# Groups of nodes that fit 17 slots of edges, found on chip, in place of blocks of 128 nodes, in a two-layer graph attention kernel

## The chip, the cores and the metric

One Trainium2 chip, one core. The metric is the device time of one execution in microseconds; a run is one execution, and the time of a kernel is the median of its runs.

## What is computed

Two layers of relational graph attention over 3125 nodes with 768 features, then a residual and a layer norm. There are 53125 edges, sorted by the node they point at (`dst`), each of one of 3 types. Every node has an edge to itself, so no node is empty; a node has 17.0 edges in the mean.

```python
def rgat_conv(x, W, q, k, b, src, dst, etype, heads, out_ch, n_nodes):
    xr = jnp.einsum('nd,rdf->rnf', x, W)          # three products per node, one per edge type
    oi = xr[etype, dst]
    oj = xr[etype, src]
    qi = oi @ q
    kj = oj @ k
    alpha = jax.nn.leaky_relu(qi + kj, NEG_SLOPE)
    m = jax.ops.segment_max(alpha, dst, num_segments=n_nodes)
    e = jnp.exp(alpha - m[dst])
    z = jax.ops.segment_sum(e, dst, num_segments=n_nodes)
    a = e / (z[dst] + EPS)
    msg = (a[:, :, None] * oj.reshape(-1, heads, out_ch)).reshape(-1, heads * out_ch)
    return jax.ops.segment_sum(msg, dst, num_segments=n_nodes) + b

h = rgat_conv(x, W1, q1, k1, b1, src, dst, edge_type, 4, 192, n)
h = jax.nn.elu(h)
out = rgat_conv(h, W2, q2, k2, b2, src, dst, edge_type, 1, 768, n)
x = _layernorm(x + out)
```

## The kernel before

The nodes are cut into NB = 25 blocks of P = 128 (the last has 53). Since the edges are sorted, the edges of a block stand together. They are taken in slots of 128 edges, one edge per partition: SL = 18 slots for each of the first 24 blocks, SLL = 9 for the last, NK = 441 in all. A block with more edges than its slots hold raises `flag`, and then a general kernel, which stands behind a test at the end of the program, does everything again.

The order of the instructions on every engine is written out by hand (`tc.manual_schedule`). What the program says first on an engine runs first there. A dictionary `ev` lists what is to be issued at each step of a pass.

**Preparation** (`prepare`, `weights_kq`, `nodes_kq`). The edge lists are brought to DRAM (`ed_d`: source row, scaled target, type, and whether the target changes; `dr_d`: target modulo 128). For each of the 26 block borders DVE counts the edges that lie before it (L205), so that `starts` holds where each block's edges begin. Meanwhile W1 is split into two parts of short mantissa (`wH`, `wL`), and each node's attention keys and queries for all types and heads are worked out: keys go to a table `kt1` in DRAM, queries to `qq` in SBUF. `first` makes block 0's rows of the first table.

**Pass 1** (`phase1`). Its steps n are the products of x with W1, `d_group(b, r, c)`: block b, type r, half c of the 768 outputs, 18 matmuls of 128x384 each (L629). Six of them make a block's rows of the first table `tab1`; ACT copies each out of PSUM (L641), SP stores them (L643). There are 144 steps and a few behind them. Between them stands the attention of layer 1. For block b, counted from step 6b: `a_load` (its edge list, SP) and `a_load2` at -9; `a_index` (a PE transpose, L516) at -6; `a_index2` (DVE makes the gather list `ridx`, L520 to L526) and 18 gathers of keys (`a_gathers`, POOL, L451, into one of three tiles `kt`) at -5; `a_q`, `a_q2`, `a_q3` (each edge's query, by a product of a one-hot matrix with the block's queries) at +1 to +3; `a_alpha` (DVE, L565, which needs all keys of the block) at +4; `a_max`, `a_scan` (maxima over each node's edges by two scans), `a_back`, `a_put` (weights into `pall`) at +5 to +8. For the blocks below 8, the steps from +4 on come two later. The last block has a list of its own (`last`), since pass 2 begins with it. W2 is split and stored beside this, and loaded over W1's place in the last 24 steps.

**Pass 2** (`phase2`). Its steps k are the slots. `gather(k)` (POOL, L451) brings 128 rows of 772 numbers of `tab1` into one of nine tiles `share`. `high` scales them by the weights per head (ACT, L788) and makes the 0/1 matrix `sel` that adds edges to nodes (POOL, L790, in two slots of three; DVE in the third). `low` makes the rest of the scaled rows (DVE, L802). `sums` adds into the block's PSUM (PE, L821, four matmuls). When a block is complete, e_y to e_s2 apply bias and ELU and transpose it, and `d_part` multiplies it with W2 (PE, L876, 108 matmuls, 18 parts spread over the slots of the next block). `d_row` copies the rows out (L884) and SP stores them in `tab2` (L890). The blocks go in the order 24, 0, 1, ..., 23.

**Pass 3** (`phase3`). The same over `tab2` for layer 2, with the attention of a block (a_load to a_put) worked out between the slots. The rows go into six tiles `G` of six slots (PART). The sums (L1090) follow the gathers by LAG = SL + 11 slots. At the end of a block the residual is added, normalised (e_y to e_low), and SP stores the result (`e_out`, L1130).

All gathers are issued by one helper, so they have one line:

```python
G.indirect_dma_start(out=to, out_offset=None, in_=tab, in_offset=_index(i[:, j:j + 1]), ...)   # L451
steps = ((-9, a_loads), (-9, a_loads2), (-6, a_index), (-5, a_index2), (-5, a_gathers), (1, a_q), (2, a_q2),
         (2, a_window), (3, a_q3), (4, a_alpha), (5, a_max), (6, a_scan), (7, a_back), (8, a_put))
order = [NB - 1, *range(NB - 1)]       # pass 2
LAG = SL + 11                          # pass 3
```

Of the kernel before, what the change touches and what calls it, by code (L numbers as in the profile page):

```python
# [37 lines left out]
SL = 18  # L38
CAP = SL * P

SLL = 9

FRONT = 256
BACK = CAP + 256

PART = 6
# [5 lines left out]
def kernel(  # L52
# [8 lines left out]
):  # L61

# [26 lines left out]
    NK = (NB - 1) * SL + SLL  # L89
# [5 lines left out]
    first_rows = {0: 0, 1: 1, 2: 2, NB - 1: 3}  # L95
# [4 lines left out]
    tab2 = dram.tile([NP * R, RW], F32, name="ftab2")  # L100
    kt1 = dram.tile([NP * R, 4], F32, name="kt1")
    xb_d = dram.tile([NP, D], F32, name="xb_d")
# [11 lines left out]
    starts = keep.tile([1, 32], I32, name="starts")  # L114
# [3 lines left out]
    dl = keep.tile([P, NB, SL], F32, name="fdl")  # L118
    rel = keep.tile([P, NB, SL], F32, name="rel")
    pall = keep.tile([P, NB, SL, H1], F32, name="pall")  # L120
    q1s = keep.tile([P, NB, H1, R, 3], BF, name="q1s")
# [48 lines left out]
    def prepare(work, bank, wide, half):  # L170
# [7 lines left out]
        cnt = work.tile([EP, 32], F32, name="cnt")  # L178
        V.memset(cnt, 0.0)
# [20 lines left out]
        blk = tile_(I32)  # L200
        V.tensor_single_scalar(blk, di, 7, op=ALU.logical_shift_right)
        bb, junk, dr = (half[:EP, i * ET:(i + 1) * ET] for i in range(3))
        V.tensor_copy(bb, blk)
        for b in range(NB + 1):
            V.tensor_scalar(junk, bb, float(b), 0.0, op0=ALU.is_lt, op1=ALU.add, accum_out=cnt[:, b:b + 1])  # L205
            yield
            if b == 10:
                win = wide[:EP, :ET + P]
                c = ed_d[1:2, FRONT:FRONT + 1]
                G.dma_start(win, bass.AP(tensor=c.tensor, offset=c.offset, ap=[[ET, EP], [1, ET + P]]))  # L210
                rx = tile_(F32)
                V.scalar_tensor_tensor(rx, si, float(R), ti, op0=ALU.mult, op1=ALU.add)
                store(ed_d[0], rx)
                yield
                tf = tile_(F32)
                V.tensor_copy(tf, ti)
                store(ed_d[2], tf)
                yield
                V.tensor_single_scalar(di, di, P - 1, op=ALU.bitwise_and)
                V.tensor_copy(dr, di)  # L220
                store(dr_d[0], dr)
                yield
# [3 lines left out]
        V.tensor_reduce(cnt[:, 30:31], junk, AX.X, ALU.add)  # L226
        yield
        V.tensor_tensor(junk, dB, win[:, P:ET + P], op=ALU.is_equal)
        V.tensor_reduce(cnt[:, 31:32], junk, AX.X, ALU.add)
# [8 lines left out]
        T.matmul(pc[:1, :32], ones, cnt, start=True, stop=True)  # L238
        cf = work.tile([1, 32], F32, name="cf")
        V.tensor_copy(cf, pc[:1, :32])  # L240
        V.tensor_copy(starts, cf)
        yield
        big = work.tile([1, 32], F32, name="big")
        V.tensor_sub(big[:, :NB], cf[:, 1:NB + 1], cf[:, 0:NB])
        V.tensor_scalar(big[:, :NB - 1], big[:, :NB - 1], float(CAP), None, op0=ALU.is_gt)
        V.tensor_scalar(big[:, NB - 1:NB], big[:, NB - 1:NB], float(SLL * P), None, op0=ALU.is_gt)
        V.tensor_copy(big[:, 30:32], cf[:, 30:32])
        V.memset(big[:, NB:30], 0.0)
        tot = work.tile([1, 1], F32, name="tot")
        V.tensor_reduce(tot, big, AX.X, ALU.add)  # L250
        V.tensor_copy(flag, tot)
# [90 lines left out]
    def nodes_kq(buf, pre, work, psum, bank, wk, kqs, wH, wL, qq, more, edges_ready):  # L342
# [86 lines left out]
        for m in range(1, NCH + 2):  # L429
            if m >= NCH:  # L430
                place(m - 2, prod.pop(m - 2))
            elif m > 1:
                got[m] = turn(m)
            fill(fills[m])
            if 0 <= m - 1 < NCH:
                prod[m - 1] = product(m - 1, got[m - 1])
            more(3)
            if m == NCH - 3:
                edges_ready()
                x_load(pre, 1)  # L440
        yield

    ends = {min((b + 1) * SL, NK) - 1 for b in range(NB)}
# [1300 lines left out]
```

## Time and profile before

| | us |
|---|---|
| median of three runs | 2289.55 |
| lowest and highest run | 2287.75, 2296.72 |
| the profiled execution | 2285.11 |
| its span, from the first to the last instruction | 2283.3 |
| first gather of keys | 124.46 |
| first sum of pass 2 | 743.85 |
| first gather of pass 3 | 1608.82 |

Busy time over the span: PE 2049.8 us (90%), PE's weight loads 1765.0 (77%), DVE 1555.7 (68%), ACT 1401.7 (61%), POOL 1733.3 (76%). The mean granted clock of PE was 0.95 of full speed.

How to read the lines that follow: "L451 POOL DMA_INDIRECT kt<-kt,ridx x378 | busy, mean ns | idle before <-what ended it" is a group of like instructions; a gather through `rfirst` instead of `ridx` is the same operation for blocks 0, 1, 2 and 24. A line of the waits is "engine line waited for: total us, times, longest us". In a timeline a line begins with the start and the duration in us. PE is TensorE, PEld its weight loads, DVE VectorE, ACT ScalarE, POOL GpSimd, SPq the queue of SyncE.

### The profile page before, as it was taken

The page shows a single profiled execution, that of the slowest core. Times are in us where ns is not written, and L with a number is a line of the kernel's source. Part 1 is how long each engine was busy: PE and PEld are TensorE (multiplying, and loading weights), DVE is VectorE, ACT ScalarE, POOL GpSimd, SP SyncE. Part 2 cuts the span into 40 slices and gives each one's busy share as a digit, 9 for nine tenths or more (in the row PEclk, how much of TensorE's full clock was granted, in tenths as well). Part 3 has the DMA queues.
Part 4 walks back from the last instruction along what each step waited for, and adds up shares of the span by engine and source line. Part 5 has one row for each costly group of instructions (what it writes and reads, how often), then busy time and mean ns, then how long its engine had stood idle before and what let it go on. Part 6 is the DMA issues. An engine that isn't in the chain of part 4 may idle for free.

```text
span 2283.3 us, 37563 instructions
## 1 busy us (share of the span) xinstructions
PE 2049.8 (90%) x11055; PEld 1765.0 (77%) x11055; DVE 1555.7 (68%) x4075; ACT 1401.7 (61%) x3197; POOL 1733.3 (76%) x1685
## 2 busy tenths in 40 slices
PE   6998988898886899999999999999489999899986
PEld 5888888888886799999999999999255555565554
DVE  7734434343432899999999999996266666676666
ACT  5411111111111788888888888885278888787885
POOL 4267777777776888888888888884677777777772
PEclk9989998999998899999999999999699999999998
DMA  6554544454455877777777777776788888888881
GB/s 181 178 149 164 170 145 145 161 170 145 159 184 158 308 245 234 233 230 235 234 235 237 228 233 240 236 233 219 256 283 298 298 306 299 288 273 281 278 289 65
DMA packets 153595, 508.22 MB, mean 223 GB/s; under 512 B 40404, under 2 KB 53723, under 8 KB 153383
## 3 DMA queue, kind: packets, MB, share of 16 engines
q0 software_dynamic: 85472, 334.19, 48.2%
q1 hardware_dynamic: 57681, 155.56, 19.0%
q10 hardware_dynamic: 10230, 15.98, 2.2%
q8 instruction: 91, 1.49, 0.3%
q14 instruction: 121, 0.99, 0.1%
HBM read 428.40 MB, written 94.04 MB: 229 GB/s over the span
## 4 chain that ended last, share of the span: by engine, by line
PE 38%; POOL 7%; DMA 6%; issue 6%; DVE 6%; ACT 4%; POOLq 0%; DVEq 0%; ACTq 0%
PE po L876 14%; PE acc L821 11%; PE acc L1090 10%; DMA G<-ftab,ridx 5%; POOL share L451 3%; POOL sel L790 2%; DVE L L802 2%; POOL G L451 1%; ACT H L1068 1%; DVE L L1079 1%; PE pt L851 1%; DMA G<-ftab,rfirst 1%; DMA share<-ftab,ridx 1%; PE pa L1020 0%; PE bc L977 0%
## 5 line engine op out<-in xcount | busy, mean ns | idle before, releaser
L788 ACT ACTIVATE H<-share,pall 128x193 fp32r<-128x193 f32 x1748 | 642.7, 447 | 104.9 <-DMA share<-ftab,ridx 36.6
L802 DVE SCALAR_TENSOR_TENSOR L<-share,pall,H 128x193 fp32r<-128x193 f32 x1748 | 648.6, 437 | 25.2 <-ACT H L788 17.7
L876 PE MATMUL po<-wH,hT 128*128 128x386 f32 (+1 forms) x1800 | 532.8, 339 | 0.0
L451 POOL DMA_INDIRECT G<-ftab,ridx x378 | 421.9, 1116 | 115.2 <-issue 58.8
L451 POOL DMA_INDIRECT kt<-kt,ridx x378 | 405.2, 1072 | 115.1 <-issue 113.9
L451 POOL DMA_INDIRECT share<-ftab,ridx x378 | 428.1, 1133 | 81.3 <-DVE L L802 42.0
L629 PE MATMUL po<-wH,xT 128*128 128x384 f32 x1584 | 444.1, 353 | 0.7 <-ACT xT L615 0.7
L1090 PE MATMUL acc<-G,selp 128*128 128x386 f32 x904 | 357.0, 521 | 0.3 <-ACT selp L1064 0.3
L876 PEld LDWEIGHTS po<-wH,hT 128*128 128x128 f32 x1800 | 334.4, 189 | 0.6 <-DVE hT L864 0.5
L876 PE MATMUL po<-wL,hT 128*128 128x386 f32 (+1 forms) x900 | 304.7, 339 | 0.0
L629 PEld LDWEIGHTS po<-wH,xT 128*128 128x128 f32 x1584 | 301.3, 196 | 3.4 <-issue 0.8
L641 ACT COPY share<-po 128x384 f32<-128x384 f32 x144 | 68.9, 479 | 337.0 <-PE po L629 267.2
L629 PE MATMUL po<-wL,xT 128*128 128x384 f32 x792 | 274.7, 347 | 0.0
L821 PE MATMUL acc<-H,sel 128*128 128x386 f32 x874 | 242.5, 359 | 20.6 <-POOL sel L790 10.9
L1079 DVE SCALAR_TENSOR_TENSOR L<-G,p,H 128x772 fp32r<-128x772 f32 x215 | 218.9, 1020 | 59.9 <-ACT H L1068 59.5
L1090 PEld LDWEIGHTS acc<-G,selp 128*128 128x128 f32 x904 | 171.6, 201 | 84.1 <-issue 19.9
L790 POOL TENSOR_SCALAR sel<-frow,fdl 128x128 fp32r<-128x128 f32 x291 | 226.1, 777 | 13.0 <-PE acc L821 1.1
L821 PE MATMUL acc<-L,sel 128*128 128x386 f32 x874 | 227.0, 341 | 0.0
L1068 ACT ACTIVATE H<-G,p 128x772 fp32r<-128x772 f32 x215 | 199.1, 928 | 3.9 <-DVE p L1044 3.8
L821 PEld LDWEIGHTS acc<-H,sel 128*128 128x128 f32 x874 | 149.6, 190 | 55.2 <-POOL sel L790 46.2
L565 DVE TENSOR_TENSOR a<-qe,kt 128x72 f32<-128x72 f32 x25 | 5.8, 233 | 242.8 <-DMA kt<-kt,ridx 213.3
L876 PEld LDWEIGHTS po<-wL,hT 128*128 128x128 f32 x900 | 169.6, 188 | 0.0
(231 smaller groups left out, 3009.7 us busy)
## 6 DMA issues: line engine op xcount, KB each, us to landing
ftab<-r SPq DMA_DIRECT2D x75, 386.0 KB
ftab<-share SPq DMA_DIRECT2D x72, 386.0 KB
sT<-dr_d SPq DMA_DIRECT2D x25, 576.0 KB
share<-in_L_gnn_W_dram SPq DMA_DIRECT2D x36, 384.0 KB
w_d<-w2hl SPq DMA_DIRECT2D x18, 768.0 KB
share<-in_x_dram SPq DMA_DIRECT2D x25, 384.0 KB
xb_d<-share SPq DMA_DIRECT2D x25, 384.0 KB
xr<-in_x_dram SPq DMA_DIRECT2D x23, 384.0 KB
```

The lines of the kernel that those rows point to most:

```text
L451: G.indirect_dma_start(out=to, out_offset=None, in_=tab, in_offset=_index(i[:, j:j + 1]), bounds_check=NP * R - 1, oob_is_err=False)
L629: T.matmul(po[:, :HALF], xT[:, s, t, :], w[:, i, sl], start=(n == 0), stop=(n == 3 * DT - 1))
L641: S.copy(to, po[:, :HALF].rearrange("p (h f) -> p h f", h=2))
L788: S.activation(H[:, c], g[:, c], AF.Copy, scale=pall[:, b, j, h:h + 1])
L790: (V if k % 3 == 0 else G).tensor_scalar(sel, row, dl[:, b, j:j + 1], None, op0=ALU.is_equal)
L802: V.scalar_tensor_tensor(L[:, c], g[:, c], pall[:, b, j, h:h + 1], H[:, c].bitcast(F32), op0=ALU.mult, op1=ALU.subtract)
L821: T.matmul(acc[:, c, :HW], sel, a[:, c * HW:(c + 1) * HW], start=(j == 0 and i == 0), stop=(k in ends2 and i == 1), skip_group_check=True)
L851: T.transpose(pt[:, t // 3, (t % 3) * P:(t % 3 + 1) * P], s["ey"][:, t * P:(t + 1) * P], ident)
L876: T.matmul(po[:, :wd], hT[:, k, t, :], w[:, r * DT + t, sl], start=(t == 0 and n == 0), stop=(t == DT - 1 and n == 2))
L1068: S.activation(H, g, AF.Copy, scale=p)
L1079: V.scalar_tensor_tensor(L, g, blk[b]["p"][:, j:j + 1], st[k][1].bitcast(F32), op0=ALU.mult, op1=ALU.subtract)
L1090: T.matmul(acc[:, c, :HW], sel, a[:, c * HW:(c + 1) * HW], start=(j == 0 and i == 0), stop=(k in ends and i == len(parts) - 1))
```

## The change

A group is no longer 128 nodes, but as many consecutive nodes, 128 at most, as have all their edges in SL = 17 slots (SLF = 14 for group 0). There are again 25 groups, and NK = 14 + 24 x 17 = 422 slots. Where a group ends depends on the edges, so it is worked out on chip, in pass 1, one group after the other: from the transposed edge list of group b, `a_next` takes the node of the first edge that no longer fits (limited by 128 nodes and by N) as the start of the next group, and `a_next2` counts the group's edges and writes the next group's first edge and first node into `starts`, from which SP reads registers for its loads and stores.

```diff
-SL = 18
+SL = 17
-SLL = 9
+SLF = 14
-PART = 6
-    NK = (NB - 1) * SL + SLL
+    NK = (NB - 1) * SL + SLF
...
+        def a_next(b):
+            s = st[b]
+            pT = s["pi"]
+            T.matmul(pT[:, 64:65], ident[0:1, 0:1].to_broadcast([1, P]), dl[0:1, b, slots(b):slots(b) + 1],
+                     start=True, stop=True)
+            n, m = (n_all[:, b + c:b + c + 1] for c in (0, 1))
+            V.tensor_scalar(m, pT[:, 64:65], n, s["lim"], op0=ALU.add, op1=ALU.min)
+            own = work.tile([P, 1], F32, name="own", bufs=2)
+            V.tensor_sub(own, m, n)
+            s["cnt"] = work.tile([P, 1], F32, name="cnt", bufs=2)
+            junk = work.tile([P, SL], F32, name="inv", bufs=2)
+            V.tensor_scalar(junk, dl[:, b, :SL], own, 0.0, op0=ALU.is_lt, op1=ALU.add, accum_out=s["cnt"])
+
+        def a_next2(b):
+            s = st[b]
+            pT = s["pi"]
+            T.matmul(pT[:, 66:67], rel3[:, 1, 0:1].to_broadcast([P, P]), s["cnt"], start=True, stop=True)
+            c, m = (slice(b + i, b + i + 1) for i in (0, 1))
+            V.tensor_scalar(s_all[:, m], pT[:, 66:67], s_all[:, c], float(E), op0=ALU.add, op1=ALU.min)
+            V.tensor_copy(starts[0:1, 0, m], s_all[0:1, m])
+            V.tensor_copy(starts[0:1, 1, m], n_all[0:1, m])
+            low = work.tile([P, 1], I32, name="low", bufs=2)
+            V.tensor_scalar(low, n_all[:, m], col, None, op0=ALU.add)
+            V.tensor_single_scalar(low, low, P - 1, op=ALU.bitwise_and)
+            V.tensor_copy(cols[:, m], low)
```

The 26 counts leave the preparation, and its pieces are spread over the steps anew. The queries go to DRAM (`q1_d`), and each group loads its own. Products with W1 still run over blocks of 128 nodes, but each third of one (six matmuls) now waits for one gather of keys:

```diff
-        for b in range(NB + 1):
-            V.tensor_scalar(junk, bb, float(b), 0.0, op0=ALU.is_lt, op1=ALU.add, accum_out=cnt[:, b:b + 1])
...
+        s["q"] = work.tile([P, H1 * R * 3], BF, name="q1", bufs=2)
+        nc.sync.dma_start(s["q"], nodes(b, q1_d))
...
-        def d_group(b, r, c):
+        def d_group(n, b, r, c):
+            g, k = divmod(n, 6)
...
-                    T.matmul(po[:, :HALF], xT[:, s, t, :], w[:, i, sl], start=(n == 0), stop=(n == 3 * DT - 1))
+                    m = T.matmul(po[:, :HALF], xT[:, s, t, :], w[:, i, sl], start=(n == 0), stop=(n == 3 * DT - 1))
+                    if n % 6 == 0:
+                        tc.add_manual_dep(m.ins, gathered[g, (3 * k + n // 6) * slots(g) // 18].name, behind,
+                                          reason="an even load")
```

The order in pass 1: the index of a group and its list (`a_index`, `a_index2`) now stand in one step, with the search for the next group behind them; the last group has no list of steps of its own. Pass 2 takes the groups in order, 0 to 24:

```diff
-        steps = ((-9, a_loads), (-9, a_loads2), (-6, a_index), (-5, a_index2), (-5, a_gathers), (1, a_q), (2, a_q2),
+        chain = ((-6, a_index), (-6, a_index2), (-5, a_gathers), (-5, a_next), (-4, a_next2))
+        for b in range(1, NB):
+            for d, f in chain:
+                ev.setdefault(6 * b + d + (b == 1), []).append((f, b))
+        steps = ((-10, a_loads), (-9, a_loads2), (1, a_q), (2, a_q2),
                  (2, a_window), (3, a_q3), (4, a_alpha), (5, a_max), (6, a_scan), (7, a_back), (8, a_put))
-        last = ((-14, a_loads), (-9, a_loads2), (-9, a_index), (-8, a_index2), (-8, a_gathers), (-4, a_q), (-3, a_q2),
-                (-3, a_window), (-2, a_q3), (-1, a_alpha), (0, a_max), (1, a_scan), (2, a_back), (3, a_put))
...
-        order = [NB - 1, *range(NB - 1)]
+        order = range(NB)
```

Rows of the second table, the residual's input and the output now lie at a group's first node, which SP reads from `starts` (`nodes`). Since 128 rows are always written, the next group's rows go over the surplus ones of this group, so a store of the output waits for the one before; the last one is a scatter on POOL. The tiles `G` of pass 3 become one tile of 36 slots:

```diff
+    def nodes(b, t):
+        if b == 0:
+            return t[0:P]
+        return t[bass.ds(nc.sync.value_load(starts[0:1, 1, b:b + 1], min_val=0, max_val=N), P)]
...
-                nc.sync.dma_start(
-                    tab2[b * P * R:(b + 1) * P * R, :].rearrange("(p r) f -> p r f", r=R)[:, r, :], o)
+                nc.sync.dma_start(nodes(b, tab2.rearrange("(n r) f -> n r f", r=R))[:, r, :], o)
...
-        gs = [work.tile([P, PART, RW], F32, name=f"G{i}", bufs=1) for i in range(NT)]
+        gs = work.tile([P, NG, RW], F32, name="G", bufs=1)
...
+            if b == NB - 1:
+                i = G.indirect_dma_start(out=out, out_offset=_index(oidx), in_=y, in_offset=None, bounds_check=N - 1,
+                                         oob_is_err=False)
+            elif b == 0:
+                i = nc.sync.dma_start(out[0:P, :], y)
+            else:
+                n = nc.sync.value_load(starts[0:1, 2, b:b + 1], min_val=0, max_val=N - P)
+                i = nc.sync.dma_start(out[bass.ds(n, P), :], y)
+            if b > 0:
+                tc.add_manual_dep(i.ins, stored[-1].name, whole_dep, reason="the next group's rows go over this one's")
```

If the nodes don't fit 25 such groups, `flag` is raised as before.

## The prediction

> **What bounds the kernel now.** I read the costliest groups first, then the table by stage, then the waits, then the timeline at the seams. The kernel has a preparation (to 124 us) and three passes over 441 slots of edges: pass 1 gathers keys, pass 2 gathers rows of the first table, pass 3 rows of the second. Every slot is one gather issued by POOL (L451):
>
> ```profile
> L451 POOL DMA_INDIRECT G<-ftab,ridx x378 | 421.9, 1116 | 115.2 <-issue 58.8
> L451 POOL DMA_INDIRECT kt<-kt,ridx x378 | 405.2, 1072 | 115.1 <-issue 113.9
> L451 POOL DMA_INDIRECT share<-ftab,ridx x378 | 428.1, 1133 | 81.3 <-DVE L L802 42.0
> ```
>
> Busy plus idle before, over 378, is 1.42 us a slot in pass 3, 1.38 in pass 1. The table by stage (busy us of PE, its weight loads, DVE, ACT, POOL, then granted clock) makes pass 2 look like PE's:
>
> ```profile
> core 0: us, PE busy (x) PEld busy (x) DVE busy (x) ACT busy (x) POOL busy (x), PEclk, DMA share, GB/s
> 124.00:425.00 301.00, 267.68 (x1644) 256.73 (x1645) 123.45 (x264) 54.50 (x107) 233.82 (x220) 0.94 0.49 160
> ...
> 770.00:1100.00 330.00, 324.74 (x1793) 309.75 (x1793) 319.12 (x928) 290.37 (x786) 287.59 (x292) 1.00 0.80 245
> ...
> 1643.00:1950.00 307.00, 282.04 (x1182) 175.61 (x1183) 202.67 (x464) 248.30 (x447) 240.65 (x218) 0.94 0.88 296
> ```
>
> The waits say otherwise (who waited for whom: total us, times, longest). The first two lines are of 770 to 1577, the other two of the whole run:
>
> ```profile
> POOL share L451 <- DVE L L802: 46.9, 240, 0.3
> ...
> POOL share L451 <- issue: 21.2, 95, 0.3
> ```
> ```profile
> DVE a L565 <- DMA kt<-kt,ridx: 213.3, 22, 15.2
> ...
> POOL kt L451 <- issue: 132.5, 435, 0.3
> ```
>
> No pause of POOL's gathers is over 0.3 us: that is the cost of a next gather, not a wait. DVE in contrast waits up to 15.2 us for keys. POOL in the middle of pass 2:
>
> ```profile
> L451 POOL DMA_INDIRECT share<-ftab,ridx x158 | 178.5, 1130 | 34.0 <-DVE L L802 17.5 <-issue 8.0 <-ACT H L788 4.1
> L790 POOL TENSOR_SCALAR sel<-frow,fdl 128x128 fp32r<-128x128 f32 x106 | 83.3, 786 | 4.4
> ```
>
> That is 1.345 us a gather plus two selections in three slots at 0.827: 1.345 + 0.551 = 1.896 us a slot. Pass 2 ran from its first sum at 743.85 to its last at 1577.5: 833.6/441 = 1.890. So POOL's queue, back to back, sets the pace of all three passes, PE and DVE close behind in pass 2. The seams, in the timeline:
>
> ```profile
> 124.46 1.10 POOL L451 DMA_INDIRECT kt<-kt,rfirst  x1 [20.84 <-ACT xT L615]
> ...
> 727.68 1.00 POOL L451 DMA_INDIRECT kt<-kt,rfirst  x1 [0.30 <-issue]
> ...
> 734.57 0.32 SPq L643 DMA_DIRECT2D ftab<-share  x1
> ...
> 737.88 1.00 POOL L451 DMA_INDIRECT share<-ftab,rfirst  x1 [9.20 <-ACT e L586]
> ...
> 1608.82 1.08 POOL L451 DMA_INDIRECT G<-ftab,rfirst  x1 [36.73 <-DVE one L956]
> ...
> 2232.13 1.01 POOL L451 DMA_INDIRECT G<-ftab,rfirst  x1 [0.30 <-PE acc L1090]
> ```
>
> Keys run from 124.46 to 728.68 without a hole; the first table's gathers then wait for its last row, stored at 734.57.
>
> **The change, part by part.** Slots fall from 24x18 + 9 = 441 to 24x17 + 14 = 422, so each pass issues 19 gathers fewer. Filling groups by the rule of the diff with the reference's edges (a group ends at 128 nodes or at the node that no longer fits) closes exactly at node 3125 with the 25th group, the last with 1806 of its 2176 places used, so the kernel's own path does all the work.
>
> *Pass 1.* 604.2 us/441 = 1.370; 19 x 1.370 = **-26.0**. This needs POOL never to run dry, now that a group's start is known only when the group before has been indexed. Per group the edit adds two small PE products (0.26 us each, as the index transpose), 12 small DVE operations at 0.17 to 0.2 = 2.2 us, a register load on SP (a DMA with one takes 0.83 on SP's queue, one without 0.33) and a load of its own queries (a few KB). DVE is 41% busy in this stage, so the 2.2 us are hidden; were DVE full, they would cost 24 x 2.2 = 53. Order of the chain: the index of group b stands six products before group b's place, when PE has waited for the last key of b-2, and POOL then still has the 17 keys of b-1 to do, 23.3 us. PE needs one more product (18 x 0.1764 = 3.2) and DVE 1 us before b's list is ready, with the landing of a key (728.68 to 731.21, 2.5 us) about 7: some 16 us to spare. SP's register load waits for DVE; behind it stand the stores of table rows and the loads of x and W2, for which ACT and PE wait only through three row buffers. Their own waits on ACT are already up to 20.8 us there.
>
> The wait of each third: behind it stand six matmuls (1.06 us), then the next third, transposes and the index. A key comes each 1.37 us and 17 keys carry 18 thirds, so 1.29 us a third; PE's need per group is 108 x 0.1764 + 2.3 small = 21.4 of 23.3 us. It fits by 1.9. Cover gone, PE would bound by what it lacks. Moving the list's arithmetic into the index's own step makes DVE wait there for PE's transpose, ahead of the scan (1.9 us) and ACT's exponent; ACT then evacuates a product late, and PE, with two accumulators, loses about 0.8 us a group. Bounds: 0, or PE short by 1 us a group, +24; I take 0, nearer the rows.
>
> *Seam 1 to 2.* PE is now held to the keys, so its last product follows the last key of the group before the last; the last row is stored some 12 us before POOL ends its keys. The first table gather can issue at once. Before, first sum minus last key's end is 743.85 - 728.68 = 15.2. After: landing 2.5, then alpha 0.5, transposes 0.8, scans 1.9, exponent 0.3, back and copy 0.6, and scaling of the first slot 1.5: 7.8. **-7.4** (bounds 0 and -10).
>
> *Pass 2.* POOL alone would give 19 x 1.89 = -36. But it now starts with a group of 14 slots, not 9, so PE gets its first W2 product five slots later: 770.0 - 743.85 + 5 x 1.9 = 35.7 us in. Afterwards a group holds 17 x 4 + 108 + 6 = 182 matmuls x 0.1764 = 32.1 us of PE, and 17 x 1.896 = 32.2 of POOL; DVE, now 0.967 x 34.0 = 32.9 a block, loses one slot's 1.6 and is at 31.3. Three engines within 3%: I take 32.6 us a group, 1% over the largest. Some 16 slots are then done: 406/17 x 32.6 = 778.6, and the last products add 28 (1577 to 1605). 35.7 + 778.6 + 28 = 842 against 861 (743.85 to 1604.9): **-19**. Bounds: PE at its mean of the stage before, 834.7/4569 = 0.1827 a matmul, 33.25 a group: -3; POOL alone, -36.
>
> *Pass 3.* 624.3/441 = 1.416; 19 x 1.416 = **-26.9**. PE is at 92% busy there and follows. One tile G of 36 slots replaces six of six; if a gather had to wait for the whole tile it would stall, but wH, one tile, is reloaded in parts at 692.33 while PE multiplies from it without a pause, so waits go by parts. The tail from the last gather holds 26 slots, not 27, and the last store moves from SP (0.37) to POOL (about 1.3): 0 together.
>
> *Preparation.* The 26 counts (0.59 + 0.08 us on DVE, L205) go, some 5 us of work replace 17.7. From 33 to 59 us DVE has nearly no idle time, so the loop there gains some; from 66 on the period is 4.25 us with the counts and 4.25 after them, so nothing. **-2** (bounds +1, -6). Row stores with a register add 0.5 at seam 2 to 3: **+0.5**.
>
> Sum: -2 - 26.0 - 7.4 - 19 + 0.5 - 26.9 = **-81**. The profiled execution took 2285.1 (span 2283.3), giving 2204; it lies 4.4 below the median of the runs, so 2289.55 - 81 = **2208**.
>
> Two rules speak against this. The key gathers take 997 ns at the median and 1072 in the mean, so something now and then lengthens them by 0.4 to 0.7. The Trainium skill, SBUF — State Buffer, section "SBUF: two separate sides", says a POOL-issued DMA can't write its descriptors while DVE runs certain two-port operations; were all 2.2 us of new DVE work per group such, the sum would be 2208 + 53 = 2261. In pass 3 PE pauses 128 times by at most 0.3 us with the clock at 0.94, and it fell to 0.57 only in 724 to 744 where PE stood still. The skill, TensorE: Matmul & The Clock Gate, section "A second HAM failure mode: psum-queue depth-cycling", says frequent micro-idles make the clock swing to half; at half rate all through, 108 products would take 38 us a group and the sum would be some 2208 + 24 x 17 = 2616.
>
> **Rivals.**
> - *PE takes over.* Pass 2 gains 3 instead of 19, since 32.1 against 32.2 leaves no room for jitter: 2224; with PE short in pass 1 too (+1 us a group), 2248. For: PE at 98% and DVE at 97% busy. Against: the same engines waited little at 96.5% of their floor.
> - *Everything goes with POOL*: -36 in pass 2, -10 at the seam, -6 before: 2208 - 17 - 2.6 - 4 = 2184.
> - *The chain starves POOL* (slower). Place: the first key of each group. If a group's list came only after the keys before it had ended, the chain in series (transpose 0.3, DVE 0.9, product and DVE 0.9, product and DVE 1.3, SP 0.8, landing 2.5 to 3) costs 7 us a group: 24 x 7 = +168, 2376. It decides from 81/24 = 3.4 us of lateness a group; the 16 us to spare speak against.
> - *It falls back to the general kernel*, far slower: excluded by the filling above unless a count is off.
>
> **How the numbers follow.** Forecast 0.66 (its own range 2192 to 2222), PE takes over 0.16, all with POOL 0.08, starving 0.09, fallback 0.01. Range 2184 to 2240: it leaves out most of the starving case and the far ends of the others. No change is within 0.5%, 2278 to 2301, about what a measurement of this kernel can tell. Faster 0.87, same 0.04, slower 0.09.
>
> **What would show it.** Right: 422 gathers a pass, no POOL pause over 0.3 us inside a pass, keys ending near 701, first sum 8 us later, pass 3's gathers spanning 597. Wrong: POOL waiting on DVE lists (L523) once a group, key gathers over 1.1 us in the mean, PE's clock near half in pass 1, or pass 2 at 1.95 us a slot or more.

## The result, and the profile after

On the chip of the first measurement the changed kernel took **2189.81 us** in the median of 4 runs (2187.15 to 2195.73), the kernel before 2290.28 (2287.75 to 2296.72): a ratio of 0.9561, 95% interval 0.9542 to 0.958. That is 18 us less than the forecast of 2208, inside its range. But the gain belongs to the chip as much as to the kernel. In the experiments below chip D gave 0.9595 (0.9569 to 0.9621), and chip C, on which the kernel before takes 2527 us, gave 1.0117 (1.0023 to 1.0212): no gain, rather a small loss. First the profile of the first chip.

The gathers of the three passes, from the costliest groups of the changed kernel (busy us, mean ns, then idle time before them):

```profile
L461 POOL DMA_INDIRECT G<-ftab,ridx x374 | 424.0, 1134 | 114.0 <-issue 57.9
L461 POOL DMA_INDIRECT share<-ftab,ridx x374 | 428.3, 1145 | 80.5 <-DVE L L875 30.9
L461 POOL DMA_INDIRECT kt<-kt,ridx x374 | 396.8, 1061 | 114.2 <-issue 110.1
```

Each gather costs POOL what it cost before, within 18 ns; there are 19 fewer in each pass (374 and 48 through `rfirst`, 422 in all; before, 378 and 63, 441). The table by stage, in stretches of pass 1, 2 and 3 as long as those shown of before:

```profile
core 0: us, PE busy (x) PEld busy (x) DVE busy (x) ACT busy (x) POOL busy (x), PEclk, DMA share, GB/s
126.00:425.00 299.00, 279.82 (x1759) 264.99 (x1760) 147.24 (x423) 55.80 (x110) 232.93 (x217) 0.98 0.55 168
743.00:1073.00 330.00, 326.95 (x1847) 321.06 (x1847) 318.29 (x931) 292.29 (x788) 288.06 (x291) 1.00 0.82 250
1573.00:1880.00 307.00, 275.93 (x1152) 170.07 (x1152) 198.33 (x446) 242.32 (x438) 242.09 (x214) 0.94 0.90 302
```

In pass 1 the granted clock rose from 0.94 to 0.98, and DVE's busy time from 123 to 147 us: that is the new arithmetic of the lists (L556 to L584, 25.9 us in this stretch). Whether DVE and POOL wait for it is in the waits of pass 1 (total us, times, longest), with the last line from the kernel before:

```profile
POOL kt L461 <- issue: 123.5, 405, 0.3
DVE fdl L545 <- PE pT L540: 87.8, 24, 10.5
DVE a L634 <- DMA kt<-kt,ridx: 71.0, 13, 6.7
```
```profile
DVE fdl L520 <- PE pT L516: 14.7, 13, 2.2
```

DVE now waits six times as long for PE's index transposes (87.8 us for 14.7) and a third as long for keys (71 for 213), but POOL's pauses between gathers are still 0.3 us each (one of 0.5): the new waits lie beside the gathers. The seam between pass 1 and pass 2, in the timeline:

```profile
700.83 1.00 POOL L461 DMA_INDIRECT kt<-kt,ridx  x1 [0.30 <-DMA ftab<-share]
...
702.13 0.99 POOL L461 DMA_INDIRECT share<-ftab,rfirst  x1 [0.30 <-issue]
...
705.82 0.23 DVE L634 TENSOR_TENSOR a<-qe,kt 128x68 f32<-128x68 f32 x1 [5.32 <-DMA share<-ftab,rfirst]
...
711.05 1.39 PE L894 MATMUL acc<-H,sel 128*128 128x386 f32 x2 [0.89 <-ACT H L861]
```

The first row gather follows the last key by 0.3 us (9.2 before), and the first sum comes 9.2 us after the keys' end (15.2 before). The end of the run:

```profile
2145.01 0.99 POOL L461 DMA_INDIRECT G<-ftab,ridx  x1 [0.30 <-issue]
...
2147.69 0.19 DVE L1088 TENSOR_TENSOR a<-qe,G 128x17 f32<-128x17 f32 x1 [3.71 <-DMA G<-ftab,ridx]
...
2178.00 1.07 POOL L1208 DMA_INDIRECT out_dram<-xb,oidx  x1 [8.74 <-ACT xb L1206]
```

Cutting both traces at the same events (first and last key, first sum, last product with W2, first and last gather of pass 3, end) gives the terms of the forecast as they were measured:

| term | forecast, us | first chip, us |
|---|---|---|
| preparation (first key 124.5 -> 126.2) | -2 | +1.7 |
| pass 1 (keys 604.2 -> 575.6) | -26.0 | -28.6 |
| seam 1 to 2 (15.2 -> 9.2) | -7.4 | -6.0 |
| pass 2, first sum to last product (861.1 -> 826.2) | -19 | -34.9 |
| seam 2 to 3 (3.9 -> 4.2) | +0.5 | +0.3 |
| pass 3's gathers (624.3 -> 604.6) | -26.9 | -19.7 |
| tail (50.2 -> 39.4) | 0 | -10.8 |
| sum | -81 | -98 (spans 2283.3 -> 2185.4) |

### The profile page after: what moved, and what is told of

It reads as the page before. It is cut to its first block, busy times and chain, and to the rows that moved or that the text cites. A ratio compares the mean times of both kernels' runs of the same rounds, so it can differ in the third digit from the quotient of the medians.

```text
span 2185.4 us, 37792 instructions
## 1 busy us (share of the span) xinstructions
PE 1994.7 (91%) x10953; PEld 1736.7 (79%) x10953; DVE 1528.2 (70%) x4159; ACT 1358.0 (62%) x3095; POOL 1669.4 (76%) x1615
## 3 DMA queue, kind: packets, MB, share of 16 engines
q0 software_dynamic: 81904, 331.52, 50.2%
## 4 chain that ended last, share of the span: by engine, by line
PE 52%; DMA 14%; issue 14%; POOL 13%; DVE 4%; ACT 2%; POOLq 0%; DVEq 0%; SPq 0%; ACTq 0%
PE po L949 21%; PE acc L894 13%; POOL kt L461 9%; DMA G<-ftab,ridx 9%; PE acc L1168 8%; PE po L698 4%; DMA kt<-kt,ridx 2%; POOL G L461 2%; PE bank L282 1%; PE pt L260 1%; DVE L L1157 1%; PE po L396 1%; PE pt L924 1%; POOL share L461 1%; ACT H L1146 1%
## 5 line engine op out<-in xcount | busy, mean ns | idle before, releaser
L861 ACT ACTIVATE H<-share,pall 128x193 fp32r<-128x193 f32 x1672 | 616.9, 447 | 91.2 <-PE acc L894 29.6
L875 DVE SCALAR_TENSOR_TENSOR L<-share,pall,H 128x193 fp32r<-128x193 f32 x1672 | 621.0, 437 | 16.5 <-issue 6.6
L461 POOL DMA_INDIRECT G<-ftab,ridx x374 | 424.0, 1134 | 114.0 <-issue 57.9
L461 POOL DMA_INDIRECT kt<-kt,ridx x374 | 396.8, 1061 | 114.2 <-issue 110.1
L1168 PE MATMUL acc<-G,selp 128*128 128x386 f32 x868 | 341.5, 519 | 0.0
L698 PEld LDWEIGHTS po<-wH,xT 128*128 128x128 f32 x1584 | 292.8, 190 | 19.8 <-ACT share L713 7.0
L1157 DVE SCALAR_TENSOR_TENSOR L<-G,p,H 128x772 fp32r<-128x772 f32 x205 | 208.2, 1017 | 57.3 <-ACT H L1146 56.9
L894 PE MATMUL acc<-H,sel 128*128 128x386 f32 x836 | 224.9, 350 | 12.1 <-POOL sel L863 10.9
L863 POOL TENSOR_SCALAR sel<-frow,fdl 128x128 fp32r<-128x128 f32 x278 | 216.0, 777 | 12.6 <-PE acc L894 1.8
L894 PE MATMUL acc<-L,sel 128*128 128x386 f32 x836 | 217.3, 341 | 0.0
L1146 ACT ACTIVATE H<-G,p 128x772 fp32r<-128x772 f32 x205 | 189.9, 928 | 0.9 <-DVE p L1122 0.8
L894 PEld LDWEIGHTS acc<-L,sel 128*128 128x128 f32 x836 | 154.8, 191 | 0.2 <-DVE L L875 0.2
```

The lines of the kernel that those rows point to most:

```text
L461: return G.indirect_dma_start(out=to, out_offset=None, in_=tab, in_offset=_index(i[:, j:j + 1]), bounds_check=NP * R - 1, oob_is_err=False)
L698: m = T.matmul(po[:, :HALF], xT[:, s, t, :], w[:, i, sl], start=(n == 0), stop=(n == 3 * DT - 1))
L861: S.activation(H[:, c], g[:, c], AF.Copy, scale=pall[:, b, j, h:h + 1])
L863: (V if k % 3 == 0 else G).tensor_scalar(sel, row, dl[:, b, j:j + 1], None, op0=ALU.is_equal)
L875: V.scalar_tensor_tensor(L[:, c], g[:, c], pall[:, b, j, h:h + 1], H[:, c].bitcast(F32), op0=ALU.mult, op1=ALU.subtract)
L894: T.matmul(acc[:, c, :HW], sel, a[:, c * HW:(c + 1) * HW], start=(j == 0 and i == 0), stop=(k in ends2 and i == 1), skip_group_check=True)
```

## The experiments

There are twelve runs, in four jobs, each job on another chip. The kernel before was timed beside them in each job and tells the chips apart: 2486 us on chip B, 2527 on C, 2289 on D, 2521 on E; chip A is that of the result (2290); its number is not on record, so it may be one of the others. No chip was used in two of the four jobs: whether a difference between them belongs to the chip, or to the state that it was in at the time, was not tested, and "chip" below means a chip in its job. Where a pass is compared across runs of one chip, its length runs from the start of its first gather to the start of its last.

**1. Without the waits of each third.** The edit, in d_group:

```diff
-                    if n % 6 == 0:
-                        tc.add_manual_dep(m.ins, gathered[g, (3 * k + n // 6) * slots(g) // 18].name, behind, ...)
```

> The changed kernel without the waits that hold each third of a product with W1 behind one gather of keys; nothing else is changed. Theory (POOL's row of gathers sets the time of pass 1, PE is beside it): the 422 keys again take 575 us (1.364 us each) and the time stays within 3 us of 2190; only PE's granted clock in pass 1 falls from 0.98 towards the 0.95 of before. Rival (the even load is what made pass 1 shorter, through the clock): keys and products come late by what PE loses, 3% of its 533 busy us, some 16 us, time about 2206. Second rival (the waits themselves cost POOL or PE time): 5 us or more faster, 2185 or below.

Chip B: 2494.67 us, 1.004 (1.0004 to 1.0077) of the kernel before. None of the three held, because the pass itself was another: 815.2 us for the keys instead of 575, at a clock of 0.81 to 0.86. The runs beside it show that the missing waits are not the reason: variants that keep them (3 and 4 below) needed 830.3 and 830.8 us for the same keys. Their pass is 15 us longer, in one trace of each.

**2 to 4. One small gather more in each of 24 groups, in one pass at a time.** The edit in pass 3 (in pass 2 the same; in pass 1 behind a group's own gathers):

```diff
             gather_rows(gs[:, k % NG, :], tab2, b, j)
+            if b and j == 8:
+                gather_rows(more_k[:, b], kt1, b, 0)
```

> The changed kernel with one more gather of keys (16 bytes for each of 128 edges, into a tile that nobody reads) behind each group's gathers in pass 1, 24 in all. Theory (POOL's queue is the bound of pass 1): 24 x 1.364 = +33 us, time 2223, the pass 608 us. Rival (PE's products, or the chain of list, products and loads, set the pass and POOL has room): under +10 us, time below 2200.

> The changed kernel with one more small gather (16 bytes for each of 128 edges, into a tile that nobody reads) in the middle of each of 24 groups of pass 2. Theory A (POOL's queue sets pass 2, as it did before): 24 x (1.06 busy + 0.3 to the next) = +33 us, time 2223. Theory B (PE, which was busy for 506.5 of 509 us, sets pass 2 and POOL has room of at least a gather in a group): under +10 us, time below 2200. Between them: POOL has some room and then binds, +10 to +25.

> The changed kernel with one more small gather (16 bytes for each of 128 edges) in the middle of each of 24 groups of pass 3: a whole instruction for POOL, one two-hundredth of a row gather's bytes for the DMA engines. Theory (POOL's queue sets pass 3): 24 x (1.06 + 0.3) = +33 us, time 2223. Rival (the DMA engines, busy for 0.89 of the pass at 298 GB/s, set it, so that POOL has room): under +10 us, time below 2200.

Medians 2533.22, 2525.84 and 2541.32 us, all on chip B, so they are read pass by pass. The last of them, by the line that issues the gathers (minimum, median and maximum ns, then first and last start):

```profile
L461 POOL DMA_INDIRECT G<-ftab,ridx x374: 992/998/2718, 1894.9 to 2488.1; - x187
...
L461 POOL DMA_INDIRECT G<-ftab,rfirst x48: 992/998/2007, 1821.2 to 1893.6; - x48
```

*Pass 3* ran from 1821.2 to 2488.1, 666.9 us; in the three other runs 628.1, 636.0 and 631.4. 24 gathers of 16 bytes an edge cost 35.1 us, 1.46 each (1.3 to 1.6 by the scatter of the three), as much as a row gather's place. So POOL's queue sets pass 3, not the bytes: the DMA engines' busy share between 1900 and 2400 us fell to 0.84 as the pass grew longer (0.86 and 0.87 in the other runs). *Pass 2*: 826.9 against 800.2, 802.8 and 804.8: +24.3, where each added gather took 1.24 us at the median and 0.3 to the next, 37 in all. POOL had room for a third of them; the case between the theories. *Pass 1*: 851.5 against 830.3 and 830.8: +21, which is neither 33 nor under 10, in a pass whose POOL stands still for 258 us waiting for lists. The theory that POOL's queue is the bound there is false on this chip.

**5. The changed kernel itself again.**

> The changed kernel itself, for the runs beside it and to see whether its gain holds on another chip. On the chip of the runs so far, where the kernel before took 2486 instead of 2290 us, pass 1 of three variants lasted 815 to 852 us (575 in the changed kernel's profile) at a granted clock near 0.82. Theory (that chip grants less clock to PE in pass 1, which then sets the pass, and the change's gain there is lost): on such a chip about 2500 less the added gathers, 2490 to 2510, no faster than before; on a chip like the first, 2190. Rival (the added gathers or the missing waits made pass 1 slow): 2190 wherever the kernel before takes 2290, and 95% of the kernel before on a chip where that is slow.

Chip C: 2549.25 us (2536.59 to 2554.67), the kernel before 2526.52, ratio 1.0117 (1.0023 to 1.0212). The rival fell: nothing had been added, and pass 1 took 867.3 us. Of the theory the loss of the gain came true, but not its number (2490 to 2510), and its cause, the clock, is by the timeline further down not the main one. Pass 1 of this run, by table and waits:

```profile
126.00:985.00 859.00, 650.15 (x3299) 563.64 (x3299) 267.91 (x768) 101.38 (x205) 434.75 (x415) 0.81 0.37 114
```

```profile
POOL kt L461 <- DVE lim L556: 292.4, 22, 22.3
```

And of run 8, whose pass 1 is that of the kernel before, on the same chip:

```profile
126.00:875.00 749.00, 563.20 (x3123) 520.25 (x3122) 229.76 (x494) 100.85 (x198) 458.78 (x435) 0.85 0.38 122
```

```profile
POOL kt L451 <- DVE rel L526: 163.7, 22, 22.8
```

This is the picture that the forecast gave for its slower rival, "the chain starves POOL": POOL waits for the list in 22 groups, 13.3 us each after the change and 7.4 before it. Pass 1 with 422 keys takes 867.3 us, with 441 keys 756.7. The 19 gathers fewer save 26 us, the waits cost 129 more: +103 of the +110.6 measured. The rest of the kernel still gains: seam, pass 3 and tail are 15.7, 28.7 and 5.8 us shorter than in run 8.

What PE loses lies for the most part in one product of each group, ahead of the transposes that begin the next list: the second behind the small products of the query terms. From its first matmul to its last it takes over 4 us in 22 of 23 groups, 10.1 at the median and 15.2 at most; in the changed kernel on chips A and D it takes 3.1 at most. Over the pass that is 179 of the 293 us by which it is longer than on A. The timeline of PE in run 5 (start, duration), with the 17 small products of the query terms (L613) and the two products with W1 behind them:

```profile
399.55 0.58 PE L613 MATMUL pq<-q,sT 128*128 128x36 bf16 x17
399.97 0.42 PE L698 MATMUL po<-wH,xT 128*128 128x384 f32 x1
...
403.04 0.33 PE L698 MATMUL po<-wH,xT 128*128 128x384 f32 x1
403.75 0.28 PE L659 MATMUL pa<-fident,e 68*128 68x68 f32 x1 [0.37 <-issue]
405.24 0.33 PE L698 MATMUL po<-wH,xT 128*128 128x384 f32 x1 [1.21 <-ACT share L713]
406.69 0.33 PE L698 MATMUL po<-wL,xT 128*128 128x384 f32 x1 [1.12 <-issue]
407.44 0.42 PE L698 MATMUL po<-wH,xT 128*128 128x384 f32 x1 [0.42 <-issue]
```

The first product runs its 18 matmuls from 399.97 to 403.2, at 0.176 us as elsewhere. The second takes from 405.24 to 418.8: most of its matmuls start 0.7 or 1.4 us apart, four or eight times as far. The granted clock in that stretch:

```profile
406.00:408.00 2.00, 0.75 (x2) 0.33 (x2) 1.25 (x4) 0.00 (x0) 1.70 (x2) 1.00 0.86 328
...
410.00:412.00 2.00, 1.84 (x4) 0.81 (x3) 0.00 (x0) 0.00 (x0) 1.65 (x2) 0.50 0.12 29
```

The matmuls are as far apart at clock 1.00 as at 0.50, so in this product the clock's halving comes with the slow pace but does not make it. On chips B and E too this product takes over 4 us in most groups of the changed kernel's variants (medians 6.2 to 10.1). In run 8 PE loses its time in another form: 24 gaps of over 3 us between matmuls, 127 us in all, where run 5 has 4 (19 us), and 62 us at distances of 0.6 to 1.6 us, where run 5 has 242. A caution: the traces of B, C and E hold some 20,000 semaphore events, those of A and D 37,000, so what is named there as having ended a wait ("issue", "DVE lim") is less certain than usual; the lengths of the waits come from the starts of instructions. Whether the recording itself, which loses events there, holds PE was not tested either.

**6. The missing waits again, beside the changed kernel.** The edit is that of run 1.

> The changed kernel without the waits of each third of a product on a gather of keys, a second time, beside the changed kernel. On a chip with a granted clock near 1 in pass 1: theory (POOL sets the pass) within 5 us of the changed kernel; rival (the even load keeps the clock up) 10 us or more slower, with the clock in pass 1 down from 0.98. On a chip with the clock near 0.82 in pass 1: PE sets the pass, the waits can only hold it back, 10 to 20 us faster than the changed kernel.

2548.64 us against 2549.25, not the 10 to 20 us less that were expected; pass 1 860.3 us against 867.3, clock as low. PE's slow products stay without the waits. The waits of each third neither cause nor cure the slow pass: single traces put them at 7 us of it on chip C and 15 on B, the medians on C at nothing. What they bring on a chip like A was not tried; there is only the clock of pass 1, 0.98 with them and 0.95 in the kernel before.

**7. A fifth of PE's matmuls left out in pass 2.**

```diff
-                for n, (k, w) in enumerate(((0, wH), (0, wL), (1, wH))):
+                for n, (k, w) in enumerate(((0, wH), (1, wH))):
...
-                             stop=(t == DT - 1 and n == 2))
+                             stop=(t == DT - 1 and n == 1))
```

> The changed kernel with a third of the products with W2 left out in pass 2 (those of the weights' low halves): 146 instead of 182 matmuls a group, 6.4 us less of PE in each of 25 groups. Theory A (POOL's queue, with DVE beside it, sets the pace of pass 2): within 10 us of the changed kernel. Theory B (PE sets it): 25 to 60 us faster, until DVE (488 of 509 busy) or POOL is the bound. The end of the pass, where the last group's products stand alone, gives some 6 us in both.

2550.27 us. Pass 2 took 807.8 us; in runs 5 and 6 on the same chip 793.8 and 809.0. Theory A: with 146 matmuls a group instead of 182, PE only waits more, and it is for POOL, in 1100 to 1700:

```profile
PEld acc L894 <- POOL sel L863: 123.0, 163, 3.0
...
POOL share L461 <- issue: 29.1, 124, 0.3
```

**8. The kernel before, without POOL's selections in pass 2** (a constant tile, `one_sel`, stands in their place)**.**

```diff
-            sel = work.tile([P, P], F32R, name="sel", bufs=4)
-            (V if k % 3 == 0 else G).tensor_scalar(sel, row, dl[:, b, j:j + 1], None, op0=ALU.is_equal)
+            sel = one_sel
+            if k % 3 == 0:
+                sel = work.tile([P, P], F32R, name="sel", bufs=4)
+                V.tensor_scalar(sel, row, dl[:, b, j:j + 1], None, op0=ALU.is_equal)
```

> The kernel before, without the selections that POOL makes in pass 2 (two of three slots; a constant tile stands in their place), so that POOL's need falls from 1.896 to about 1.345 us a slot. Theory A (POOL alone set the pace before): 1.890 us a slot falls to PE's need, 186 matmuls x 0.1764 / 18 = 1.823, or to DVE's, so 441 x 0.067 = some 30 us faster than the kernel before. Theory B (PE set it already): within 10 us. Its passes 1 and 3 are those of the kernel before and serve as such on this chip.

2539.13 us, 1.0086 (1.0041 to 1.0131). Theory B said within 10 us; it is 12.6 slower. The rows come at 1.895 us a slot, 1.883 in the kernel before on chip A. POOL in 1100 to 1500, first in this run, then in the kernel before:

```profile
L451 POOL DMA_INDIRECT share<-ftab,ridx x210 | 270.2, 1287 | 130.8 <-DVE L L806 43.0 <-ACT H L790 34.6 <-issue 21.5
```

```profile
L451 POOL DMA_INDIRECT share<-ftab,ridx x213 | 239.8, 1126 | 45.8 <-DVE L L802 23.7 <-issue 10.8 <-ACT H L788 6.3
```

Relieved, POOL pauses for 131 of 400 us (its longest pause 3.8 instead of 0.3) and the pace does not change. So theory A falls: POOL did not set the pace alone. Runs 7 (of the changed kernel) and 8 (of the kernel before) together say that in pass 2 at least two engines stand level. The second is probably PE, busy for 385 of these 400 us, but relieving both in one kernel was not tried.

**9 to 11. The changed kernel once more as the mark, the small products spread, and, with them spread, a shorter first group.** The edit of 10, in which one(j) is the matmul taken out and q_one(1) issues the next of those left, and what 11 adds (its start of pass 3's query terms moved by a few slots, so that the shorter group fits):

```diff
-            for j in range(SL):
-                T.matmul(pq[...], s["sT"][:, j * P:(j + 1) * P], s["q"], start=True, stop=True)
+            between.extend((one, j) for j in range(SL))
...
                 for s, w in ((0, wH), (0, wL), (1, wH)):
                     m = T.matmul(po[:, :HALF], ...)
+                    q_one(1)
```
```diff
-SLF = 14
+SLF = 11
```

> The changed kernel itself once more, as the mark for the two runs beside it. On a chip where the kernel before takes 2290 us: 2190, keys 1.365 us apart, no product longer than 4 us behind the 17 small products of a group's query terms. On a chip where the kernel before takes 2480 to 2530: 2500 to 2550, keys 1.97 to 2.06 us apart, and in each group one product with W1 that takes 8 to 15 us instead of 3.2, starting 3.1 us after those 17 small products, with the granted clock at half behind it.

> The changed kernel with the 17 small products of a group's query terms (128x36 results, 0.03 us apart, 0.6 us in all) put one behind each of the 17 first matmuls of the product that follows, instead of all ahead of it; nothing is left out. Theory (on a chip with slow pass 1, this burst is what holds PE for 8 to 15 us in every group, and the list of the next group, which POOL waits for, stands behind it): the slow products are gone, keys come at 1.37 to 1.5 us, and the time falls by 200 to 250 us against the changed kernel there. On a chip like the first: within 5 us of 2190. Rival (the slow product comes from PE's own pause behind it, for the copy of a product by ACT, and from the clock's halving): the slow products stay where they are, and the time is within 30 us of the changed kernel on any chip.

> The kernel with the spread small products and a first group of 11 slots instead of 14 (25 groups still hold all edges, by the filling rule), so 419 instead of 422 gathers a pass. Theory (each gather issued costs its pass POOL's pace): 3 x (1.37 + 1.89 + 1.43) = 14 us less than the kernel with the spread alone. Rival (the first group is hidden behind the start of each pass): within 4 us of it.

Chip D is like A: 2192.12 (0.9595, 0.9569 to 0.9621), 2197.56 (0.9599, 0.9563 to 0.9636) and 2200.99 us (0.9634, 0.9605 to 0.9664). The mark repeats the result. With no slow products to take away, the spread could show nothing of its theory, which **stays open**. Its time is 7.6 us above the 2190 that was expected to within 5, so it has a price: PE is busy for 549 of 560 us in pass 1 (130 to 690) against 529 in the mark. On top of that the shorter first group gained nothing of its 14 us, so the rival's number came (within 4 us). Its POOL now waits for lists, in 120 to 712:

```profile
POOL kt L461 <- DVE lim L556: 21.1, 16, 11.6
```

In the mark that wait is 2.2 us, once; with the spread alone 6.6 us, in 3. The 14.5 us more are as much as was to be gained, in one trace of each: fewer gathers are worth POOL's pace only while the list is early, and here PE, whose products stand ahead of it, is full.

**12. The shorter first group alone.**

> The changed kernel, without the spread, with a first group of 11 slots instead of 14: 419 gathers a pass. In the kernel with the spread, PE was busy for 548 of 560 us in pass 1 and POOL waited some 0.46 us in each group for the next list, so that the three gathers fewer could not show there. Theory (POOL's row of gathers sets passes 1 and 3 and stands level with PE and DVE in pass 2): 3 x (1.365 + 1.89 + 1.43) = 14 us less than the changed kernel's 2190 to 2192 on a chip where the kernel before takes 2290, ratio to the kernel before 0.950 to 0.953, with keys 1.365 us apart. Rival (the first group lies beside the start of each pass, or the list of the second group comes late because it has three keys less to hide behind): within 4 us of 2190. On a chip where the kernel before takes 2480 to 2530, pass 1 is PE's and only passes 2 and 3 can show it, 10 us.

Chip E, where the kernel before takes 2521 us: 2531.27, 1.0048 (1.0008 to 1.0088). Keys 2.063 us apart, as in run 5. The changed kernel did not run on E, so the 10 us expected from passes 2 and 3 can't be read, and whether it would gain its 14 us on a chip like A stays open. Only the changed kernel itself ran on chips of both kinds.

## Why the prediction was right, and where not

*On a chip like A* the forecast's mechanism is right in the main: 19 gathers fewer in each of three passes. That POOL's queue paces them is shown for pass 1 by the trace (422 gathers with pauses of 0.3 us) and for pass 3 by run 4, on chip B; in pass 2 POOL is only one of at least two (runs 2 and 8).

- **Pass 1 and the seams** came as worked out: -28.6 for -26.0, since a key gather also got 0.006 us shorter, and -6.0 for -7.4; the last keys took 4.0 us from their end to their first use, not 2.5. The reading that a DMA with a register load "takes 0.83 on SP's queue" was wrong, without consequence: before, the load of `sT` (L477) goes by a register too and takes 0.37 us; in the changed kernel a row store by a register (L963) takes 0.33, the register's own load 0.27. The signs named for right are there: 422 gathers a pass, no pause inside a pass (the longest wait for a list 0.5 us, once), keys ending at 701.83. Two came off the mark: the first sum 9.2 us later for 8, and pass 3's gathers spanning 604.6 us for 597.
- **Pass 2 was mis-sized**: -34.9 for -19. The step that failed is "I take 32.6 us a group, 1% over the largest". Measured from the first product with W2 (742.97) to the last sum (1509.8), 406 slots took 766.8 us, 32.1 a group: three engines within 3% cost no allowance. That is 12 of the 16 us missed; the start took 31.9 us instead of 35.7, the other 4. The bound "POOL alone, -36" was the better value, though not for its reason. First and last starts, in us, are behind the durations:

```profile
L949 PE MATMUL po<-wH,hT x1800: 331/338/687, 743.0 to 1537.0; 128*128 128x386 f32 x90, 128*128 128x384 f32 x90
...
L894 PE MATMUL acc<-L,sel x836: 332/339/547, 712.2 to 1509.8; 128*128 128x386 f32 x168
```

- **Pass 3 and the tail were parted wrongly**: -19.7 and -10.8 for -26.9 and 0. Together -30.5 against -26.9. The row gathers took 1134 ns in the mean instead of 1116, so each term of 1.416 was too short by 0.017; the forecast let the pace stand. The tail's 0 was wrong in all three of its pieces, by the two traces: the last gather's first use comes 1.7 us after its end instead of 4.2, then the sums take 25.4 us instead of 30.6 (105 matmuls from the last gather on instead of 121), then 12.3 us remain instead of 15.4. No experiment took these apart.
- **Preparation**: -2 forecast, +1.7 measured, neither clear of the scatter: over the runs with this same preparation the first key starts between 121.7 and 126.8 us. DVE's busy time there fell from 87.1 to 72.1 us and bought nothing.

*On chips like B, C and E* the forecast fails, at one step: "PE needs one more product (18 x 0.1764 = 3.2) and DVE 1 us before b's list is ready [...] some 16 us to spare". The spare time was priced with a product of 3.2 us; there one product a group takes up to 15, and the list, which PE's next transposes begin, is 13 us late (run 5). Why that product is slow stays open. The rival with this mechanism was priced at 7 us a group (2376) and given a chance of 0.09. Two of the signs named for wrong (POOL waiting for lists once a group, a low clock in pass 1) are exactly what its traces show. The kernel before has late lists on such a chip too, 7.4 us each with PE standing still rather than creeping, and why the change makes them 13.3 us late is not settled: the waits of each third are not it (run 6); the chain of count, register load and load of the next group's edges, which only the changed kernel has, was not taken apart. The chance of a chip of that kind was in no view of the profile of before, which had been taken on a chip of the other kind; that the first measurement fell on a chip of the faster kind is luck.

The rule that the forecast set aside, in the Trainium skill, TensorE: Matmul & The Clock Gate, section "A second HAM failure mode: psum-queue depth-cycling", would have given 2616 by frequent micro-idles and a clock at half. The forecast set it aside because the clock "fell to 0.57 only in 724 to 744"; that reading was wrong, since the same view has 0.53 from 1605 to 1643, where PE stood still too, and there were 12 stretches at half in pass 1 (the last section). The other rule, priced at 2261, left no sign: with DVE's new work a key gather took 1061 ns in the mean, 1072 before. On A and D no run shows so long a time; on C the time was 2549 with a mean clock of 0.81 in pass 1, so its sign was there, though run 5 shows matmuls at the same slow pace with the clock at 1.00.

## What to carry to other kernels

Count what a queue has to issue: where one engine issues back to back with pauses of 0.3 us, the time follows the number of its instructions as long as no other engine stands level, and a cheap extra instruction of the same kind in each group tests that in one run (pass 3 paid 1.46 us for each, whatever its bytes). Before a table known in advance is replaced by one that the loop makes as it goes, price the spare time of the new chain with the slowest product that any chip shows, not with the mean of one trace. Run a change on more than one chip before believing a gain that rests on one engine being just fast enough.

## What the runs showed of the hardware

- **The same program takes 2190 us in two measurements (A and D) and 2549 in a third (C)**, and most of the difference lies in one stage: of 349 us between the profiles of A and C pass 1 has 293, pass 3 35. On C matmuls that elsewhere start 0.176 us apart start 0.7 or 1.4 us apart for up to 15 us at a time, once a group, behind a burst of 17 small products. Why is open: spreading the burst was only run on a chip without the effect.
- **The clock can halve after short pauses.** In windows of 2 us of the changed kernel on chip A, around a pause of PE from 338.3 to 340.96:

```profile
338.00:340.00 2.00, 0.28 (x2) 0.00 (x0) 0.00 (x0) 0.48 (x1) 1.63 (x2) 1.00 0.37 119
...
342.00:344.00 2.00, 2.00 (x8) 2.00 (x7) 0.63 (x1) 0.00 (x0) 1.53 (x2) 0.50 0.29 97
...
346.00:348.00 2.00, 2.00 (x12) 1.84 (x12) 1.53 (x6) 0.00 (x0) 1.44 (x2) 1.00 0.63 218
```

  A pause of 2.7 us is followed by 3.4 us at half clock (341.8 to 345.3). The length of the pause does not decide it alone: on chip D one of 2.0 us (from 519.9) was followed by 3.4 us at half, while in the kernel before four of 2.4 to 2.6 us (from 418.5, 494.0, 544.1 and 619.3) were not. From 126 to 702 the kernel before has 12 such stretches (55 us in all), the changed kernel 5 (26 us), and on chip C 29 in its longer pass (338 us up to 990). The Trainium skill, TensorE: Matmul & The Clock Gate, section "HAM oscillation — how this bites in real kernels", gives the rule as no idle gaps of PE over about 3.4 us; here 2.7 us sufficed, and on D 2.0.
